# Graph attention before a diffusion layer: adjacency fetched by row tile in the second head group, row sums later and in quarters, SP and ScalarE in written order

## The chip, the cores and the metric

One core of a Trainium2 chip. The engines are TensorE (PE, its weight loads PEld), VectorE (DVE), ScalarE (ACT) and GpSimd (POOL); SyncE (SP) issues DMA transfers. Each runs its own instructions in the order in which they stand in its queue, and a waiting instruction holds what stands behind it. The metric is the device time of one execution in microseconds. Before the change it is 3462.85 us, the median of three executions (3461.5 to 3477.28).

## The reference

Two graph layers on 2708 nodes with 512 features and a dense 0/1 adjacency of 2708 x 2708 floats. The first is graph attention with 8 heads of 64:

```python
h = relu(layernorm(x)); feats = einsum('nf,hfd->hnd', h, W)
dense = leaky(e_self[:, :, None] + e_neigh[:, None, :]) + NEG_INF * (1 - adj)
x = x + relu(einsum('hnm,hmd->hnd', softmax(dense), feats) + b)
```

The second (two steps of diffusion) needs S = adj + I, the sums of its rows and of its columns, and a nucleus-sampled attention of its own. What follows concerns the first layer, and three things that the first layer makes for the second while it has the adjacency at hand: S in memory (`s_d`), row sums and column sums.

## The kernel before

**Tiles.** The nodes make NT = 22 row tiles of P = 128 (the last has 20). The attention stage works on the transposed adjacency: rows m are neighbours, columns n are the nodes that get an output. The columns are cut into four chunks (`tchunks`) of TC = 6 tiles, 768 columns (WC); the last chunk has 404. The 8 heads make two groups (`hgroups`) of four.

**The main loop.** For each chunk, for each head group, for each row tile t: VectorE makes four tiles e (L477), one per head, as max(r_b, kk) times a_c, where r_b holds the shares of the chunk's columns, spread over all partitions, kk is a number per neighbour and head, and a_c is the adjacency of this row tile and chunk in bf16. TensorE multiplies them by the features fw (L483) into six PSUM banks, `po`, which accumulate over all 22 row tiles. There are exactly six banks in the pool, so the next group can start in a bank only after ScalarE has copied that bank to `o_t` (L490). There are seven buffers for e, so VectorE can be almost two row tiles ahead of TensorE.

**The fetch of a chunk** (L444 to L459), once per chunk, used by both groups: SP loads the 128 x 768 piece of the transposed adjacency into a_f (L452, four buffers); ScalarE copies it to a_c (L454, NT + 2 = 24 buffers) and adds up the column sums on the way; where the row tile lies in the chunk itself, GpSimd adds the identity to the diagonal block of a_f (L458); SP stores a_f to `s_d` (L459). Where the last chunk or the last tile leaves columns or rows over, GpSimd clears them first (L449, L451).

**r_b** (`shares`, L353) is a load of four rows, spread to 128 partitions: 1536 KB, two buffers.

**The row sums** (`row_sums`, L337): for each row tile two halves of 1354 columns of the adjacency, loaded by SP into one buffer (L345) and added up by ScalarE (L346); GpSimd adds the halves and notes rows without any neighbour (`lone`, L347 to L349). `lone` is needed when the tile is finished, and the sums for the scales `rinv` and `ratio` (L514 to L517), which the second layer uses.

**Finishing a tile** (`finished`, L359) is cut into stages: transpose `o_t` (L372), divide (`shared`), add x and take the moments (`normed`), `cleared`, `asked`, `answered`. They use all engines. The dictionary `later` gives each stage and each row sum a row tile of the main loop, counted over both groups (key gi * NT + t), after whose matmuls it is written: tile i of a chunk is finished at keys 3i to 3i + 6 of the next chunk, so in that chunk's first group. The last chunk's four tiles are finished after the loop. Row sums of a chunk's tiles stand at keys NT + 3i, in the chunk's second group.

**What sets the order.** In this stage a planner orders the instructions of each engine from its own estimate of times, so the order on an engine is not the written one: it hoists loads, and it puts the fetch of the following chunk among the second group's work, since the program does not forbid it. The two steps of the second layer stand in a block (L1296) with a written order on four engines.

Of the kernel before, what the change touches and what calls it, by code (L numbers as in the profile page):

```python
# [9 lines left out]
F32 = mybir.dt.float32  # L10
BF16 = mybir.dt.bfloat16
# [3 lines left out]
AF = mybir.ActivationFunctionType  # L15
# [10 lines left out]
P = 128  # L26
# [28 lines left out]
def kernel(  # L55
# [163 lines left out]
    with ExitStack() as l0:  # L219
# [116 lines left out]

        def row_sums(t):  # L337
            pr = rows[t]
            half = small.tile([P, 2], F32, name="half")
            w = -(-N // 2)  # L340
            for i in range(2):
                arow = adjp.tile([P, w], F32, name="arow", bufs=1)
                c = slice(i * w, min((i + 1) * w, N))
                arow = arow[:pr, :c.stop - c.start]
                nc.sync.dma_start(out=arow, in_=adj[cols[t], c])  # L345
                nc.scalar.activation(arow, arow, AF.Copy, accum_out=half[:pr, i:i + 1])  # L346
            nc.gpsimd.tensor_tensor(rsum[:pr, t:t + 1], half[:pr, 0:1], half[:pr, 1:2], op=OP.add)  # L347
            nc.gpsimd.tensor_scalar(lone[:pr, t:t + 1], rsum[:pr, t:t + 1], 0.0, None, op0=OP.is_equal)
            nc.gpsimd.tensor_scalar(lone_n[:pr, t:t + 1], lone[:pr, t:t + 1], float(N), None, op0=OP.mult)  # L349

# [85 lines left out]

        later = {}
        unasked = []
        for ci, tiles in enumerate(tchunks):
            n0, n1 = tiles[0] * P, min((tiles[-1] + 1) * P, N)  # L440
            cw = n1 - n0
            r_bs = [shares(grp, n0, cw) for grp in hgroups[:1]]
            a_c = []
            for t in range(NT):  # L444
                pr = rows[t]
                a_f = adjp.tile([P, WC], F32, name="a_f", bufs=4)
                wide = len(tiles) * P
                if pr < P:
                    nc.gpsimd.memset(a_f, 0.0)  # L449
                elif cw < wide:  # L450
                    nc.gpsimd.memset(a_f[:, cw:wide], 0.0)  # L451
                nc.sync.dma_start(out=a_f[:pr, :cw], in_=adj_t[cols[t], n0:n1])  # L452
                a_c.append(adjp.tile([P, WC], BF16, name="a_c", bufs=NT + 2))
                nc.scalar.activation(a_c[t][:pr, :cw], a_f[:pr, :cw], AF.Copy,  # L454
                                     accum_out=cpart[:pr, t, ci:ci + 1])
                if t in tiles:
                    d = slice(t * P - n0, t * P - n0 + pr)
                    nc.gpsimd.tensor_tensor(a_f[:pr, d], a_f[:pr, d], ident[:pr, :pr], op=OP.add)  # L458
                nc.sync.dma_start(out=s_d[t * P:(t + 1) * P, n0:n0 + wide], in_=a_f[:, :wide])  # L459
            for i, t in enumerate(tiles):  # L460
                later.setdefault(NT + 3 * i, []).append(lambda t=t: row_sums(t))
            r_bs += [shares(grp, n0, cw) for grp in hgroups[1:]]
            o_t = work.tile([P, NG, len(beside), WC], F32, name="o_t", bufs=1)
            halfs = -(-cw // 512)
            hw = -(-cw // halfs)
            parts = [(a, min(a + hw, cw)) for a in range(0, cw, hw)]
            w = P // HG
            for gi, (grp, r_b) in enumerate(zip(hgroups, r_bs)):
                po = [[ps_o.tile([P, 512], F32, name="po") for _ in parts] for _ in beside]
                for t in range(NT):  # L470
                    pr = rows[t]
                    es = []
                    for k, slots in enumerate(beside):
                        while len(es) <= max(i for i, _ in slots):
                            i = len(es)
                            es.append(tp.tile([P, WC], F32, name="e", bufs=7))
                            nc.vector.scalar_tensor_tensor(es[i][:pr, :cw], r_b[:pr, i, :cw],  # L477
                                                           kk[:pr, t, grp[i]:grp[i] + 1],
                                                           a_c[t][:pr, :cw], op0=OP.max, op1=OP.mult)
                        for n, (a, b) in enumerate(parts):  # L480
                            for q, (i, d) in enumerate(slots):
                                of = fw[:pr, t, grp[i], d:min(d + w, DV)]
                                nc.tensor.matmul(po[k][n][q * w:(q + 1) * w, :b - a],  # L483
                                                 lhsT=of if d < DH else of.to_broadcast([pr, w]),
                                                 rhs=es[i][:pr, a:b], start=(t == 0), stop=(t == NT - 1))
                    for stage in later.pop(gi * NT + t, ()):
                        stage()
                for k in range(len(beside)):
                    for n, (a, b) in enumerate(parts):
                        nc.scalar.copy(o_t[:, gi, k, a:b], po[k][n][:, :b - a])  # L490

            final = ci == len(tchunks) - 1
            for i, t in enumerate(tiles):
                if final and i < 3:
                    bank = lambda g: ps_o.tile([P, 512], F32, name="po")
# [990 lines left out]
```

## Time and profile before

The profile is of one execution of 3462.71 us; its span from first to last instruction is 3460.9 us.

| | |
|---|---|
| time, median of three | 3462.85 us |
| profiled execution | 3462.71 us, span 3460.9 us |
| busy: TensorE, VectorE | 3183.6 us (92%), 2573.5 us (74%) |
| busy: ScalarE, GpSimd | 1502.3 us (43%), 933.6 us (27%) |
| mean granted TensorE clock | 0.973 |
| attention matmuls (L483), first to last start | 139.5 to 923.0 us |
| e (L477) | 704, 659.7 us |
| copies of adjacency (L454), first to last start | 88, 137.5 to 768.0 us |
| row sums on ScalarE (L346), first to last start | 44, 188.1 to 480.6 us |
| SP's load of r_b (L353) | 8, 64.9 to 775.9 us |

Times within the profile count from the first instruction. A line of the page's groups gives the source line, the engine, the operation with output and inputs, how many there were, their busy time and mean duration, and after the second bar how long the engine was idle just before them and what ended most of that. A line of a timeline gives the start, the duration (of several that are merged, from the first start to the last end), the engine and line, and in brackets the idle time ahead and what ended it. "SPq" lines are issues of DMA transfers, not the transfers themselves. TensorE runs a float32 matmul as two records.

### The profile page before, as it was taken

To read this page: it belongs to the slowest core of one execution; us is meant where nothing else is said; L and a number is where in the kernel's file an instruction comes from. 1 tells how busy PE (TensorE), PEld (TensorE's weight loads), DVE (VectorE), ACT (ScalarE), POOL (GpSimd) and SP (SyncE) were. 2 spreads that over 40 slices of the span, in tenths; PEclk is the share of its full clock that TensorE was granted. 3 is DMA by queue.
4 is the path that set the end of the run, shared out by engine and by line. 5 is a ranking of instruction groups with operands and counts; after the bars stand their busy time and mean duration, and the time that the engine had idled before them with its cause. 6 is when DMAs were issued, how large, how long until landed. Compare 5 with 4: busy or idle time off the path is not lost. (4 is left out here: it accounts for less than half of the span.)

```text
span 3460.9 us, 44356 instructions
## 1 busy us (share of the span) xinstructions
PE 3183.6 (92%) x16033; PEld 1695.6 (49%) x16033; DVE 2573.5 (74%) x4485; ACT 1502.3 (43%) x2219; POOL 933.6 (27%) x1091
## 2 busy tenths in 40 slices
PE   7988899998888999999999998899988999998998
PEld 4543333332455446455564643555555555555553
DVE  4588899899857564463745634997999899898893
ACT  2333231111046766665657622346544564455510
POOL 4221743607221222122122312111321233122211
PEclk9998999999999999999999999999999999999999
DMA  4478554222386245254453534865544653556553
GB/s 135 153 240 271 188 176 146 85 93 87 114 291 222 92 143 206 67 187 165 140 181 122 199 124 141 281 220 189 188 137 139 207 200 125 175 182 220 182 178 123
DMA packets 240046, 580.65 MB, mean 168 GB/s; under 512 B 32863, under 2 KB 66107, under 8 KB 239657
## 3 DMA queue, kind: packets, MB, share of 16 engines
q1 hardware_dynamic: 217721, 503.38, 43.9%
q0 software_dynamic: 22064, 74.09, 5.6%
q8 instruction: 127, 2.08, 0.2%
q14 instruction: 134, 1.10, 0.1%
HBM read 471.68 MB, written 105.68 MB: 167 GB/s over the span
## 5 line engine op out<-in xcount | busy, mean ns | idle before, releaser
L1168 PE MATMUL a<-va,at 128*128 128x512 f32 (+2 forms) x1936 | 887.2, 598 | 4.7 <-ACT at L1150 4.6
L483 PE MATMUL po<-e,fw 128*32 128x384 f32 (+3 forms) x7392 | 675.7, 502 | 65.7 <-DVE e L477 38.7
L477 DVE SCALAR_TENSOR_TENSOR e<-r_b,kk,a_c 128x768 f32<-128x768 f32 (+3 forms) x704 | 659.7, 997 | 50.4 <-PE po L483 41.8
L604 ACT ACTIVATE junk_a<-p,nth 128x2708 uint8<-128x2708 f32 (+1 forms) x240 | 612.7, 2553 | 38.1 <-POOL nth L619 33.6
L1042 PE MATMUL q<-hl,s_r 128*128 128x512 f32 x1936 | 541.5, 426 | 70.8 <-DMA s_r<-s_d 49.8
L1168 PEld LDWEIGHTS a<-va,at 128*128 128x128 f32 (+2 forms) x1936 | 338.2, 186 | 373.8 <-issue 341.4
L1042 PEld LDWEIGHTS q<-hl,s_r 128*128 128x128 f32 x1936 | 365.1, 193 | 235.5 <-issue 67.2
L483 PEld LDWEIGHTS po<-e,fw 128*32 128x32 f32 (+1 forms) x7392 | 256.9, 112 | 449.7 <-issue 260.0
L1150 ACT COPY at<-t 128x512 f32<-128x512 f32 (+3 forms) x308 | 140.9, 478 | 652.4 <-PE t L1146 648.6
L683 DVE SCALAR_TENSOR_TENSOR junk<-p,th 128x2708 bf16<-128x2708 f32 (+1 forms) x132 | 407.3, 3086 | 3.0
L1062 PE MATMUL q<-u_k,v 128*128 128x512 f32 x704 | 316.9, 592 | 1.1 <-ACT v L1052 1.1
L1045 PE MATMUL q<-s_r,hl 128*128 128x512 f32 (+1 forms) x1056 | 279.7, 409 | 17.7 <-DMA s_r<-s_d 15.1
L1045 PEld LDWEIGHTS q<-s_r,hl 128*128 128x128 f32 x1056 | 193.2, 189 | 97.7 <-issue 49.9
L1062 PEld LDWEIGHTS q<-u_k,v 128*128 128x128 f32 x704 | 133.3, 190 | 158.9 <-issue 154.2
L570 PE MATMUL t<-keys,q_t 128*128 128x452 f32 x528 | 158.7, 424 | 52.4 <-ACT p L572 50.6
L572 ACT COPY p<-t 128x452 f32<-128x452 f32 (+2 forms) x264 | 131.5, 537 | 172.0 <-PE t L570 128.0
L879 DVE MAX8 vn<-keep 128x8 f32<-128x2708 f32 (+1 forms) x66 | 196.8, 2981 | 2.3
L597 DVE TENSOR_REDUCE nmx<-p 128x1 f32<-128x2708 f32 (+1 forms) x44 | 130.5, 2967 | 63.9 <-ACT p L572 63.9
L1215 PE MATMUL a<-u_k,v_t 128*128 128x512 f32 (+1 forms) x352 | 170.2, 624 | 4.7 <-ACT yo L1222 3.0
L155 POOL TENSOR_SCALAR ln_rs<-ln_mv 128x1 f32<-128x1 f32 x66 | 49.6, 752 | 412.8 <-DVE ln_mv L154 411.5
L1146 PEld LDWEIGHTS t<-ident,keep 128*128 128x128 f32 (+1 forms) x968 | 115.5, 139 | 77.5 <-issue 48.0
L1146 PE MATMUL t<-ident,keep 128*128 128x128 f32 (+1 forms) x968 | 146.0, 273 | 3.5 <-ACT p L572 2.8
(311 smaller groups left out, 3435.3 us busy)
## 6 DMA issues: line engine op xcount, KB each, us to landing
hl<-vhl_d SPq DMA_DIRECT2D x132, 512.0 KB
s_r<-s_d SPq DMA_DIRECT2D x264, 256.0 KB
hl<-fhl_d SPq DMA_DIRECT2D x132, 512.0 KB
hl<-bhl_d SPq DMA_DIRECT2D x132, 512.0 KB
u_k<-in_L_gnn_U_dram SPq DMA_DIRECT2D x184, 256.0 KB
arow<-in_adj_dram SPq DMA_DIRECT2D x42, 677.0 KB
s_d<-a_f SPq DMA_DIRECT2D x66, 384.0 KB
s_r<-s_d SPq DMA_DIRECT2D x132, 192.0 KB
```

The costliest lines, as they stand in the source:

```text
L477: nc.vector.scalar_tensor_tensor(es[i][:pr, :cw], r_b[:pr, i, :cw], kk[:pr, t, grp[i]:grp[i] + 1], a_c[t][:pr, :cw], op0=OP.max, op1=OP.mult)
L483: nc.tensor.matmul(po[k][n][q * w:(q + 1) * w, :b - a], lhsT=of if d < DH else of.to_broadcast([pr, w]), rhs=es[i][:pr, a:b], start=(t == ...
L570: nc.tensor.matmul(pl[:, :c1 - c0], lhsT=q[:, i], rhs=self.keys[:, c0:c1], start=(i == 0), stop=(i == 1))
L604: nc.scalar.activation(junk[:pr], self.p[i][:pr], func, **kw)
L683: nc.vector.scalar_tensor_tensor(self.junk_b[:pr], p, th, p, op0=OP.is_ge, op1=OP.mult, accum_out=dst)
L879: v.max(vs, keep[0][:pr])
L1042: nc.tensor.matmul(half[j], lhsT=s_r[:, j * P:(j + 1) * P], rhs=hl[:, h], start=(c == 0 and h == 0), stop=(c == NT - 1 and h == 1))
L1045: nc.tensor.matmul(half[j][:, :w], lhsT=hl[:, h, j * P:(j + 1) * P], rhs=s_r[:, :w], start=(c == 0 and h == 0), stop=(c == NT - 1 and h == 1))
L1062: nc.tensor.matmul(half[j], lhsT=across_t[-1][k][:, j * P:(j + 1) * P], rhs=u_k, start=(start and k == 0), stop=(start and k == KD - 1))
L1146: nc.tensor.transpose(pt[:rows[c], j, :pr], keep[i][:pr, cols[c]], ident[:pr, :pr])
L1168: nc.tensor.matmul(pa[:pr], lhsT=at[:rows[c], j, :pr], rhs=va[:rows[c], c, :], start=(c == 0), stop=(c == NT - 1))
L1215: nc.tensor.matmul(pz[i][:rows[t]], lhsT=v_t[i][:, k, :rows[t]], rhs=u_k, start=(k == 0), stop=(k == KD - 1))
```

## The change

Four things. `row_sums` takes quarters of 677 columns with two buffers instead of halves with one, with one more addition on GpSimd. The fetch becomes a function for one row tile: all 22 tiles of chunk 0 are fetched ahead of its first group, and each further chunk's tile t is fetched after row tile t of the second group of the chunk ahead of it. The row sums move: in chunks 0 to 2 the chunk's first tile at key 2 NT - 4 = 40 (row tile 18 of the second group), its other tiles at keys 3i + 1 of the following chunk; the last chunk's own tiles stay at NT + 3i. The load of r_b is written one group ahead, after the first chunk's fetch for the second group. And SP and ScalarE keep the written order until the end of the stage; the other engines are still ordered by the planner.

```diff
@@ -336,15 +336,17 @@
 
         def row_sums(t):
             pr = rows[t]
-            half = small.tile([P, 2], F32, name="half")
-            w = -(-N // 2)
-            for i in range(2):
-                arow = adjp.tile([P, w], F32, name="arow", bufs=1)
+            n = 4
+            some = small.tile([P, n], F32, name="some")
+            w = -(-N // n)
+            for i in range(n):
+                arow = adjp.tile([P, w], F32, name="arow", bufs=2)
                 c = slice(i * w, min((i + 1) * w, N))
                 arow = arow[:pr, :c.stop - c.start]
                 nc.sync.dma_start(out=arow, in_=adj[cols[t], c])
-                nc.scalar.activation(arow, arow, AF.Copy, accum_out=half[:pr, i:i + 1])
-            nc.gpsimd.tensor_tensor(rsum[:pr, t:t + 1], half[:pr, 0:1], half[:pr, 1:2], op=OP.add)
+                nc.scalar.activation(arow, arow, AF.Copy, accum_out=some[:pr, i:i + 1])
+            nc.gpsimd.tensor_tensor(some[:pr, :2], some[:pr, :2], some[:pr, 2:], op=OP.add)
+            nc.gpsimd.tensor_tensor(rsum[:pr, t:t + 1], some[:pr, 0:1], some[:pr, 1:2], op=OP.add)
             nc.gpsimd.tensor_scalar(lone[:pr, t:t + 1], rsum[:pr, t:t + 1], 0.0, None, op0=OP.is_equal)
             nc.gpsimd.tensor_scalar(lone_n[:pr, t:t + 1], lone[:pr, t:t + 1], float(N), None, op0=OP.mult)
 
@@ -436,36 +438,61 @@
 
         later = {}
         unasked = []
+        spans = [(tiles[0] * P, min((tiles[-1] + 1) * P, N)) for tiles in tchunks]
+        a_cs = [[] for _ in tchunks]
+        r_bs = [[] for _ in tchunks]
+
+        def fetched(ci, t):
+            n0, n1 = spans[ci]
+            tiles, cw, pr = tchunks[ci], n1 - n0, rows[t]
+            a_f = adjp.tile([P, WC], F32, name="a_f", bufs=4)
+            wide = len(tiles) * P
+            if pr < P:
+                nc.gpsimd.memset(a_f, 0.0)
+            elif cw < wide:
+                nc.gpsimd.memset(a_f[:, cw:wide], 0.0)
+            nc.sync.dma_start(out=a_f[:pr, :cw], in_=adj_t[cols[t], n0:n1])
+            a_c = adjp.tile([P, WC], BF16, name="a_c", bufs=NT + 2)
+            a_cs[ci].append(a_c)
+            nc.scalar.activation(a_c[:pr, :cw], a_f[:pr, :cw], AF.Copy, accum_out=cpart[:pr, t, ci:ci + 1])
+            if t in tiles:
+                d = slice(t * P - n0, t * P - n0 + pr)
+                nc.gpsimd.tensor_tensor(a_f[:pr, d], a_f[:pr, d], ident[:pr, :pr], op=OP.add)
+            nc.sync.dma_start(out=s_d[t * P:(t + 1) * P, n0:n0 + wide], in_=a_f[:, :wide])
+
+        def shared_by(ci, gi):
+            n0, n1 = spans[ci]
+            r_bs[ci].append(shares(hgroups[gi], n0, n1 - n0))
+
+        gat = l0.enter_context(tc.manual_schedule(engines={SP, ACT}))
         for ci, tiles in enumerate(tchunks):
-            n0, n1 = tiles[0] * P, min((tiles[-1] + 1) * P, N)
+            n0, n1 = spans[ci]
             cw = n1 - n0
-            r_bs = [shares(grp, n0, cw) for grp in hgroups[:1]]
-            a_c = []
-            for t in range(NT):
-                pr = rows[t]
-                a_f = adjp.tile([P, WC], F32, name="a_f", bufs=4)
-                wide = len(tiles) * P
-                if pr < P:
-                    nc.gpsimd.memset(a_f, 0.0)
-                elif cw < wide:
-                    nc.gpsimd.memset(a_f[:, cw:wide], 0.0)
-                nc.sync.dma_start(out=a_f[:pr, :cw], in_=adj_t[cols[t], n0:n1])
-                a_c.append(adjp.tile([P, WC], BF16, name="a_c", bufs=NT + 2))
-                nc.scalar.activation(a_c[t][:pr, :cw], a_f[:pr, :cw], AF.Copy,
-                                     accum_out=cpart[:pr, t, ci:ci + 1])
-                if t in tiles:
-                    d = slice(t * P - n0, t * P - n0 + pr)
-                    nc.gpsimd.tensor_tensor(a_f[:pr, d], a_f[:pr, d], ident[:pr, :pr], op=OP.add)
-                nc.sync.dma_start(out=s_d[t * P:(t + 1) * P, n0:n0 + wide], in_=a_f[:, :wide])
-            for i, t in enumerate(tiles):
-                later.setdefault(NT + 3 * i, []).append(lambda t=t: row_sums(t))
-            r_bs += [shares(grp, n0, cw) for grp in hgroups[1:]]
+            final = ci == len(tchunks) - 1
+            if ci == 0:
+                shared_by(0, 0)
+                for t in range(NT):
+                    fetched(0, t)
+            if final:
+                for i, t in enumerate(tiles):
+                    later.setdefault(NT + 3 * i, []).append(lambda t=t: row_sums(t))
+            else:
+                later.setdefault(2 * NT - 4, []).append(lambda t=tiles[0]: row_sums(t))
+            if ci:
+                for i, t in enumerate(tchunks[ci - 1][1:]):
+                    later.setdefault(3 * i + 1, []).append(lambda t=t: row_sums(t))
+            a_c = a_cs[ci]
             o_t = work.tile([P, NG, len(beside), WC], F32, name="o_t", bufs=1)
             halfs = -(-cw // 512)
             hw = -(-cw // halfs)
             parts = [(a, min(a + hw, cw)) for a in range(0, cw, hw)]
             w = P // HG
-            for gi, (grp, r_b) in enumerate(zip(hgroups, r_bs)):
+            for gi, grp in enumerate(hgroups):
+                if gi + 1 < NG:
+                    shared_by(ci, gi + 1)
+                elif not final:
+                    shared_by(ci + 1, 0)
+                r_b = r_bs[ci][gi]
                 po = [[ps_o.tile([P, 512], F32, name="po") for _ in parts] for _ in beside]
                 for t in range(NT):
                     pr = rows[t]
@@ -485,11 +512,12 @@
                                                  rhs=es[i][:pr, a:b], start=(t == 0), stop=(t == NT - 1))
                     for stage in later.pop(gi * NT + t, ()):
                         stage()
+                    if gi == NG - 1 and not final:
+                        fetched(ci + 1, t)
                 for k in range(len(beside)):
                     for n, (a, b) in enumerate(parts):
                         nc.scalar.copy(o_t[:, gi, k, a:b], po[k][n][:, :b - a])
 
-            final = ci == len(tchunks) - 1
             for i, t in enumerate(tiles):
                 if final and i < 3:
                     bank = lambda g: ps_o.tile([P, 512], F32, name="po")
```

## The prediction

> **What bounds the kernel now.** The change touches only the attention stage, so I cut the span at that stage first. The groups of instructions place its matmuls (L483) from 139.5 to 923 us. The page shows who is costly there:
>
> ```profile
> L483 PE MATMUL po<-e,fw 128*32 128x384 f32 (+3 forms) x7392 | 675.7, 502 | 65.7 <-DVE e L477 38.7
> ...
> L477 DVE SCALAR_TENSOR_TENSOR e<-r_b,kk,a_c 128x768 f32<-128x768 f32 (+3 forms) x704 | 659.7, 997 | 50.4 <-PE po L483 41.8
> ```
>
> Both engines are nearly full, and the idle time is small in total: 65.7 us of TensorE. Its place matters more than its sum. The second view is busy time per stretch, cut where one head group ends and the next begins (columns: stretch, then busy us and count of PE, PEld, DVE, ACT, POOL, then granted clock, DMA share, GB/s):
>
> ```profile
> 139.50:227.00 87.50, 87.47 (x1056) 49.20 (x1056) 86.49 (x92) 29.69 (x57) 20.47 (x16) 0.98 0.83 288
> 227.00:239.30 12.30, 0.03 (x4) 0.03 (x5) 2.52 (x3) 4.06 (x8) 0.63 (x3) 0.53 0.56 189
> 239.30:328.00 88.70, 88.70 (x1056) 32.44 (x1056) 82.25 (x86) 35.00 (x68) 18.98 (x25) 0.96 0.77 254
> 328.00:346.00 18.00, 4.22 (x32) 1.06 (x32) 2.06 (x3) 8.42 (x18) 0.94 (x5) 0.50 0.91 288
> 346.00:475.30 129.30, 114.35 (x1133) 46.01 (x1133) 110.83 (x147) 39.23 (x67) 92.94 (x103) 0.95 0.56 183
> ...
> 477.30:564.20 86.90, 86.90 (x1058) 31.90 (x1057) 83.48 (x90) 23.56 (x52) 13.66 (x20) 0.98 0.56 180
> 564.20:690.40 126.20, 114.82 (x1156) 46.24 (x1156) 113.59 (x148) 12.61 (x28) 78.65 (x74) 0.96 0.25 88
> ```
>
> A group without finishing work takes 86.9 us and TensorE is full: 3.95 us for each of 22 row tiles. A first group of chunks 1 and 2 also finishes the chunk before and takes 129.3 and 126.2 us; VectorE and GpSimd set that. Two holes stand out, of 12.3 us after the first group and about 18 us after the second. At 564.2 there is no hole. The timeline of ScalarE before the first hole's end gives the cause, and TensorE's line the result:
>
> ```profile
> 237.43 1.33 ACT L346 ACTIVATE arow<-arow 128x1354 f32<-128x1354 f32 x1 [4.28 <-DMA arow<-in_adj_dram]
> ...
> 238.76 1.98 ACT L490 COPY o_t<-po 128x384 f32<-128x384 f32 x5
> ...
> 239.27 12.95 PE L483 MATMUL po<-e,fw 128*32 128x384 f32 x124 [12.28 <-ACT o_t L490]
> ```
>
> All six accumulation banks belong to the finished group, and their copies (L490) stood behind row sums that waited for their own loads. The second hole is the same queue: three copies at 340.87, three at 345.42, row sums between and ahead of them.
>
> Last I looked at how quickly a load and a store alternate on SP, since that is the order that the new code writes down. SyncE's timeline in chunk 1's second group:
>
> ```profile
> 495.78 0.33 SPq L459 DMA_DIRECT2D s_d<-a_f  x1
> 496.20 0.38 SPq L452 DMA_DIRECT2D a_f<-in_adj_t_dram  x1
> 499.61 0.33 SPq L459 DMA_DIRECT2D s_d<-a_f  x1
> 500.03 0.38 SPq L452 DMA_DIRECT2D a_f<-in_adj_t_dram  x1
> 503.55 0.33 SPq L459 DMA_DIRECT2D s_d<-a_f  x1
> ```
>
> Each store waits until its load has landed, each load is issued 0.42 us after the store ahead of it: 3.83 and 3.94 us per tile, just TensorE's 3.95. In the first group the old order escapes this: four, later three loads are issued in a row, then their stores. The tiles on the diagonal have a longer way. ScalarE and GpSimd, chunk 2's fetch:
>
> ```profile
> 517.48 0.85 ACT L454 ACTIVATE a_c<-a_f 128x768 bf16<-128x768 f32 x1 [2.93 <-DVE e L477]
> ...
> 518.50 1.12 POOL L458 TENSOR_TENSOR a_f<-a_f,ident 128x128 f32<-128x128 f32 x1 [33.95 <-ACT a_c L454]
> ...
> 519.65 0.33 SPq L459 DMA_DIRECT2D s_d<-a_f  x1
> ```
>
> The store follows 2.1 us after ScalarE began its copy, because the addition of the identity writes what ScalarE reads.
>
> **What the Trainium skill says.** "DMA: Bandwidth & Descriptors", section "Anatomy of one DMA": a wait for a semaphore is served on the issuing sequencer, not by the DMA engines. So a store that waits holds back every later load of SP; the 3.4 us gaps above agree. The same section gives a DMA some 2 us of fixed cost besides its bytes: a 384 KB load here took 3.02 us unhindered, of which 1.15 us is data at the 341 GB/s of the busiest stretch, so 1.9 us. "TensorE: Matmul & The Clock Gate", Part 1: about 3.4 us of work at half clock after an idle time; the trace has weight loads 0.64 us apart after 239.27 and 0.32 us from 245 on, so 5.7 us. "SBUF — State Buffer", "two separate sides": a GpSimd operation and a VectorE operation with two SBUF inputs exclude each other; e (0.95 us alone) took up to 2.06 us here.
>
> **The change part by part.**
> (a) Row sums leave chunk 0, but for one tile late in its second group. The copies of the first group then find ScalarE free, and the first hole's cause goes.
> (b) Fetching in written order, one tile at a time. A plain tile: from load to store the five undisturbed ones took 3.02, 3.08, 4.42, 3.41 and 3.52 us, mean 3.49; with 0.42 us to the next load 3.9 us. A diagonal tile: 3.9 + 2.1 = 6.0 us, six per chunk.
> Chunk 0 is fetched while its own first group eats it. From the first copy at 137.5 us, tile 21 is there at 137.5 + 6×6.0 + 15×3.9 = 232.0; its copy 0.9, a first e 0.95 and 3.84 us of matmuls end the group at 237.7, against 227.0 before.
> (c) r_b of group 2 is now behind all 22 fetches on SP; before it was loaded at 68.8 us. Issued at 232.5, behind the last store, 1.57 MB at 341 GB/s = 4.6 us with 2.3 us around it and 1.1 us for the store: there at 240.6. One e later TensorE starts, at 241.7: a hole of 4 us instead of 12.3, and the group starts 2.4 us *later* than before (239.3).
> (d) The next chunk's fetch, inside the second group. SP first has the load of r_b, which waits for the last e of the first group (call this S), then the fetches. From S: r_b and first tile 1.97 MB, 5.8 + 2.3 = 8.1 us; 15 plain tiles 58.5; 6 diagonal ones 36; the row sum at tile 18, of which SP waits for two quarters, 5.4 (first quarter landed 3.3, ScalarE 0.77 and 0.86 for two, an estimate along the line from 404 elements in 0.54 us to 1354 in 1.33 us, issue 0.4); last copy 0.9: 108.9 us. Only then come the copies of the banks, in the program's order. What hides it is the second group: from S (473.5 in chunk 1) to its end (564.2) 90.7 us. Excess: 18.2 us.
> At chunk 0 to 1, S is 236.7, and r_b of group 2 is still moving (1.6 us): the copies start at 347.2, TensorE at 347.7. Before, allowing for the three matmul groups done early, it stood as if it had started at 344. So +3.7 us up to here.
> At chunk 1 to 2 there was no hole: +18.
> At chunk 2 to 3 loads are 202 KB (2.45 us to the store, cycle 3.0) and four tiles are diagonal, 1.85 us more each: 5.5 + 17×3.0 + 4×4.85 + 5.4 − 3.0 + 0.7 = 79 us, within 90: 0. If it were not, it would cost its excess.
> (e) Row sums move out of chunk 1's first group (eighteen tiles down to five): 129.3 to 126.2, −3.1; the slow copies at 475.3 go, −1.3. They move into the first groups of chunks 2 and 3, five each, four GpSimd operations per tile instead of three. GpSimd is on the path there: 20 operations of 0.2 to 0.85 us, about half of it felt, +2 each, +4; bounds 0 and +10. ScalarE is held about 5.8 us by each, one in three tiles of 5.7 us; its next finishing step comes two tiles on, so hidden. VectorE's rsum, rinv and ratio at the end: under 2 us, not counted.
> Sum: 3.7 − 3.1 − 1.3 + 18 + 4 = +21.3 us. The profiled execution took 3462.71 us (span 3460.9), which is the median 3462.85 to 0.2 us: 3484.
>
> Unknown from here: whether the very first r_b stays at 64.9 us or falls behind the stage's start; that adds 0 or 4.6 us, and I take 0.
>
> **The rivals.**
> 1. *The fetch keeps pace.* With 3.0 us per plain tile, as the 202 KB loads have it, and little for the diagonal, (d) is under 90 us, both holes go: the second group would start at 233.8, chunk 1 at 321 instead of 344, −23, with (e)'s −4.4 it is 3436. Against it: three of five waits above are over 3.4 us. This is the one on the other side; it decides where the chain falls below 90.7 us.
> 2. *Half way.* Every load as quick as the two at 3.02 and 3.08 us: cycle 3.44, diagonal 5.2 with the 0.66 us addition seen once; chain 96.6, excess 6. Chunk 0's first group ends at 233.8, chunk 1 starts at 328 (−16); −16 + 6 − 4.4 + 4 = −10: 3453.
> 3. *Row sums stall the finishing work.* GpSimd waits in its order for a quarter that comes late, VectorE for GpSimd (L401 waited 20.3 us in all for L397). Some 2 us for each of 10 row sums, over (d): 3504. Chunk 1's first group, with three times as many, was only 3 us longer than chunk 2's, so I hold it small.
> If every load were as late as the 4.42 us one, the chain would be 129 us and the total near 3540; that is the far end.
>
> **How the numbers follow.** Forecast 0.58, rival 1 0.14, rival 2 0.18, rival 3 0.10. Half a per cent, 17.3 us, is about what a measurement can tell from no change. Of the forecast's cases 0.45 lie above 3480 and 0.13 within; rival 3 is slower; rival 2 is 0.10 within and 0.08 faster; rival 1 faster. So faster 0.22, same 0.23, slower 0.55. The forecast's own range is 3470 to 3510; to leave out no more than 2 in 10 it reaches to rival 2 and a part of rival 1, and to the slower loads: 3445 to 3520.
>
> **What would show it.** The hole after group 1 shrinks to some 4 us and ends on r_b, not on ScalarE. A hole of 15 to 20 us appears where chunk 1 ends, its copies released behind an a_c copy that waited for its load; the one at chunk 0's end stays. SP's stores wait for loads in all of it, the mean cycle near 3.9 and 6.0 us. VectorE waits for a_c in the first six tiles. The prediction is wrong if TensorE runs through the end of chunk 1, or if SP issues the next load before the store.

## The result, and the profile after

The changed kernel takes 3511.61 us, the median of four executions (3509.74 to 3513.09), against 3462.53 us for the kernel before on the same chip: a ratio of 1.0129, 95% interval 1.0106 to 1.0151. The forecast was 3484 us. It is slower as forecast, and by 49.1 us between the medians where 21.3 were worked out (by the ratio some 45 us; one of the four executions of the kernel before took 3477.28 us).

The page of the changed kernel, its groups of instructions (line, engine, operation, count, then busy us and mean ns, then idle time ahead and what ended it):

```profile
L510 PE MATMUL po<-e,fw 128*32 128x384 f32 (+3 forms) x7392 | 695.0, 509 | 83.9 <-DVE e L504 62.2
L504 DVE SCALAR_TENSOR_TENSOR e<-r_b,kk,a_c 128x768 f32<-128x768 f32 (+3 forms) x704 | 656.2, 990 | 75.1 <-PE po L510 48.4
```

TensorE has the same 7392 records, with 18 us more idle time in front of them and 19 us more busy time. (L510 was L483, L504 was L477.) As before, the place matters more. Busy time per stretch, cut where a head group begins (stretch, then busy us and count of PE, PEld, DVE, ACT, POOL, then granted clock, DMA share, GB/s):

```profile
139.50:242.40 102.90, 99.15 (x1056) 39.86 (x1057) 85.17 (x89) 22.54 (x48) 4.83 (x7) 0.96 0.56 185
242.40:350.40 108.00, 88.97 (x1062) 59.80 (x1062) 89.77 (x96) 24.43 (x54) 6.02 (x11) 0.90 0.54 178
350.40:486.90 136.50, 118.85 (x1162) 47.85 (x1163) 112.51 (x146) 29.17 (x71) 87.82 (x95) 0.94 0.42 141
486.90:591.90 105.00, 90.48 (x1062) 33.44 (x1062) 84.84 (x90) 26.13 (x59) 9.53 (x18) 0.89 0.53 173
591.90:727.50 135.60, 120.74 (x1162) 48.60 (x1163) 111.96 (x146) 29.10 (x71) 88.48 (x96) 0.92 0.41 138
727.50:825.60 98.10, 93.71 (x1081) 33.55 (x1081) 83.28 (x96) 22.07 (x64) 11.77 (x30) 0.93 0.43 134
```

The second groups of chunks 0 and 1 (second and fourth line) now take 108 and 105 us where TensorE has some 90 us of work. The first groups of chunks 1 and 2 (third and fifth) take 136 us, and GpSimd is busy for 88 of them. (The last stretch runs 4 us into the next group.) The DMA engines were busy for 0.56 of chunk 0's first group, 0.83 before, so it is not their bandwidth that spaces the loads.

For a common measure, here is each group from the end of the last copy of its predecessor's banks to the end of the last copy of its own, for both kernels. (The expectations quoted below cut the groups less evenly; some of their times differ from those given here by 1 to 6 us.)

| group (us) | before | after | difference | forecast |
|---|---|---|---|---|
| chunk 0, both, end at | 346.6 | 352.2 | +5.6 | +3.7 |
| chunk 1 first | 131.0 | 136.5 | +5.5 | -4.4 |
| chunk 1 second | 87.2 | 105.0 | +17.8 | +18 |
| chunk 2 first | 127.5 | 135.6 | +8.1 | +2 |
| chunk 2 second | 87.3 | 92.6 | +5.3 | 0 |
| chunk 3 first | 95.7 | 102.9 | +7.2 | +2 |
| chunk 3 second | 49.0 | 50.8 | +1.8 | 0 |
| sum | 924.4 | 975.7 | +51.3 | +21.3 |

What follows these groups gave back 2.7 us of the span. That remainder took between 2531 and 2552 us in all the runs below, so effects of a few us are read from the groups and not from the total.

The hole at the end of chunk 0, from the timeline of the changed kernel:

```profile
346.15 0.33 SPq L461 DMA_DIRECT2D s_d<-a_f  x1
...
346.21 0.84 ACT L457 ACTIVATE a_c<-a_f 128x768 bf16<-128x768 f32 x1 [2.87 <-DMA a_f<-in_adj_t_dram]
...
349.00 0.33 SPq L461 DMA_DIRECT2D s_d<-a_f  x1
...
349.08 0.84 ACT L457 ACTIVATE a_c<-a_f 20x768 bf16<-20x768 f32 x1 [1.93 <-DMA a_f<-in_adj_t_dram]
...
349.93 1.19 ACT L519 COPY o_t<-po 128x384 f32<-128x384 f32 x3
...
350.43 0.87 PE L510 MATMUL po<-e,fw 128*32 128x384 f32 x4 [9.26 <-ACT o_t L519]
```

The second group's matmuls had ended at 330.0; the banks are copied 20 us later, because the copies stand behind the last a_c copy of the next chunk's fetch, and that one waited for its load. SP's own waits between 125 and 1000 us, in the changed kernel (us in total, times, longest):

```profile
SPq L461 <- DMA a_f<-in_adj_t_dram: 274.6, 88, 8.5
SPq L346 <- ACT arow L347: 267.7, 76, 36.2
SPq L355 <- DVE e L504: 104.2, 4, 47.7
SPq L461 <- POOL a_f L460: 44.3, 22, 5.1
```

All 88 stores waited for a load, 3.1 us each. In the kernel before it was 60, and 2.0 us each:

```profile
SPq L459 <- DMA a_f<-in_adj_t_dram: 118.7, 60, 7.0
```

### The profile page after: what moved, and what is told of

It reads as the page before. It is cut to its first block, busy times and chain, and to the rows that moved or that the text cites. A ratio compares the mean times of both kernels' runs of the same rounds, so it can differ in the third digit from the quotient of the medians.

```text
span 3509.5 us, 44598 instructions
## 1 busy us (share of the span) xinstructions
PE 3213.8 (92%) x16033; PEld 1719.8 (49%) x16033; DVE 2571.6 (73%) x4485; ACT 1513.1 (43%) x2307; POOL 934.2 (27%) x1113
## 5 line engine op out<-in xcount | busy, mean ns | idle before, releaser
L510 PE MATMUL po<-e,fw 128*32 128x384 f32 (+3 forms) x7392 | 695.0, 509 | 83.9 <-DVE e L504 62.2
L504 DVE SCALAR_TENSOR_TENSOR e<-r_b,kk,a_c 128x768 f32<-128x768 f32 (+3 forms) x704 | 656.2, 990 | 75.1 <-PE po L510 48.4
L510 PEld LDWEIGHTS po<-e,fw 128*32 128x32 f32 (+1 forms) x7392 | 272.5, 113 | 469.0 <-issue 256.2
L457 ACT ACTIVATE a_c<-a_f 128x768 bf16<-128x768 f32 (+1 forms) x88 | 67.7, 770 | 288.8 <-DMA a_f<-in_adj_t_dram 251.3
```

The source lines that it names most:

```text
L510: nc.tensor.matmul(po[k][n][q * w:(q + 1) * w, :b - a], lhsT=of if d < DH else of.to_broadcast([pr, w]), rhs=es[i][:pr, a:b], start=(t == ...
```

## The experiments

The theory for the holes: load, wait and store alternate on SP, the copies of the banks stand behind the fetch on ScalarE. Its rival: what the holes cost is mainly the slow restart of TensorE after them. For the first groups the theory is that row sums delay the finishing work through GpSimd; its rivals are the loads and ScalarE's sums, and the holes themselves.

**Stores two tiles late.** The load of the next tile no longer stands behind a store that waits.

```diff
+        owed = []
+        LAG = 2
-            nc.sync.dma_start(out=s_d[t * P:(t + 1) * P, n0:n0 + wide], in_=a_f[:, :wide])
+            owed.append(lambda: nc.sync.dma_start(out=s_d[t * P:(t + 1) * P, n0:n0 + wide], in_=a_f[:, :wide]))
+            while len(owed) > (LAG if t < NT - 1 else 0):
+                owed.pop(0)()
```

> The changed kernel with one edit: SP's store of a row tile is written two row tiles later, so two loads are under way before a store waits. ScalarE's order is as it was. If SP's chain of load, wait, store is what fills the second groups, a tile costs SP about 2.4 us (0.77 MB at some 340 GB/s) instead of 3.9 or 6.0, the fetch ends before the group does, and the holes ahead of chunks 1 and 2 (20 and 16 us) go to under 2 us; the first group of chunk 0 falls from 102.9 us to about 88, its second from 108 to 88, the second of chunk 1 from 105 to 87. The first groups of chunks 1 and 2 lose another 5 us each if half-clock restart after a hole is what lengthened them (136.5 and 135.6 us); about 1 us if it was the row sums. In all about 3430 us. If instead ScalarE's written order holds the bank copies, with the a_c copies ahead of them, holes of over 10 us stay and the time is above 3490.

Measured: 3458.56 us, ratio to before 0.9985 (0.9974 to 0.9996). Both holes are gone; chunk 0 ended at 314.8 us instead of 352.2, and the second groups of chunks 1 and 2 took 87.5 us. TensorE's line through chunk 0:

```profile
140.70 177.55 PE L514 MATMUL po<-e,fw 128*32 128x384 f32 x2160 [5.88 <-DVE e L508]
```

So the chain on SP made the holes. The first groups stayed at 137.2 and 137.3 us: they had not been long because of the holes ahead of them, and the part of the expectation that rested on that (to 3430) fell. "DMA: Bandwidth & Descriptors" of the Trainium skill (Anatomy of one DMA) has waits served on the issuing sequencer; this run shows the price here, some 50 us for a store written two tiles too early.

**No addition on the diagonal.** The lines that add the identity are left out.

```diff
-            if t in tiles:
-                d = slice(t * P - n0, t * P - n0 + pr)
-                nc.gpsimd.tensor_tensor(a_f[:pr, d], a_f[:pr, d], ident[:pr, :pr], op=OP.add)
```

> The changed kernel without the addition of the identity on the diagonal tiles (this part is not computed). If the chain of load, wait and store on SP sets both holes with the lengths of the prediction, each diagonal tile falls from 6.0 to 3.9 us: the chain of chunk 1's and of chunk 2's fetch is 12 us shorter, the holes of 20 and 16 us fall to about 8 and 4, chunk 0's first group ends some 5 to 9 us earlier: total near 3512 - 24 - 7 = 3481. If the holes come from the row sum near the end or from the load of r_b, they shorten by under 4 us each: total above 3500.

Measured: 3476.67 us, ratio 1.0043 (1.0026 to 1.006). Between the groups' matmuls the hole at the end of chunk 0 fell from 20.4 to 9.7 us, that at the end of chunk 1 from 16.3 to 10.2, and chunk 0's first group ended 9.3 us earlier (233.0 against 242.3). TensorE around the first two ends:

```profile
233.51 89.63 PE L507 MATMUL po<-e,fw 128*32 128x384 f32 x1056 [1.06 <-DVE e L501]
332.79 6.52 PE L507 MATMUL po<-e,fw 128*32 128x384 f32 x48 [8.81 <-ACT o_t L516]
```

A hole also depends on how far TensorE is behind VectorE when the chain begins. The chain itself, from SP's load of r_b to the first bank copy, shows in two lines of the changed kernel, here for the fetch of chunk 2:

```profile
479.58 0.38 SPq L355 DMA_DIRECT2D r_b<-en_d  x1
...
591.43 2.30 ACT L519 COPY o_t<-po 128x384 f32<-128x384 f32 x6
```

It takes 112.0 us for chunk 1's fetch and 111.9 for chunk 2's, and 102.6 and 103.3 without the addition. The diagonal tiles' longer way is thus 9.4 and 8.6 us of it, some 1.5 us a tile where 2.1 were expected. The rest is mostly the plain chain.

**The second group's r_b earlier in chunk 0.**

```diff
                 for t in range(NT):
                     fetched(0, t)
+                    if t == NT // 2:
+                        shared_by(0, 1)
...
                 if gi + 1 < NG:
-                    shared_by(ci, gi + 1)
+                    if ci:
+                        shared_by(ci, gi + 1)
```

> The changed kernel, but in chunk 0 the load of r_b for the second group is written after row tile 11 instead of behind all 22 fetches. If the prediction's term (c) holds, the hole of 4 us between chunk 0's two groups goes, as the fetch is one load of 5 us later on SP in its middle: the first group ends up to 5 us later or, where TensorE is behind the fetch by less, as much later as the second group starts earlier: between 0 and -4 us on the total, 3508 to 3512. If the hole has another cause (the copies of the banks, or a_c), it stays at 3 to 4 us and the total is 3512 to 3516.

Measured: 3521.25 us, ratio 1.0155 (1.0123 to 1.0187). TensorE now runs through the boundary, but it gets there 5 us later, since the load stands in the middle of the fetch instead of at its end:

```profile
224.60 37.83 PE L513 MATMUL po<-e,fw 128*32 128x384 f32 x432
```

Chunk 0 ended at 356.7 us instead of 352.2. The wait that r_b caused was in the end 0.7 us of TensorE, not 4, and moving it cost more than it held. The stage ended 3.9 us later in all; the rest of the 10 us between the medians is not in these groups.

**No row sums at all, and row sums without their GpSimd operations.** In the first kernel `row_sums` does nothing; in the second it loads and lets ScalarE add up, and the four operations after that are left out.

```diff
-            nc.gpsimd.tensor_tensor(some[:pr, :2], some[:pr, :2], some[:pr, 2:], op=OP.add)
-            nc.gpsimd.tensor_tensor(rsum[:pr, t:t + 1], some[:pr, 0:1], some[:pr, 1:2], op=OP.add)
-            nc.gpsimd.tensor_scalar(lone[:pr, t:t + 1], rsum[:pr, t:t + 1], 0.0, None, op0=OP.is_equal)
-            nc.gpsimd.tensor_scalar(lone_n[:pr, t:t + 1], lone[:pr, t:t + 1], float(N), None, op0=OP.mult)
```

> The changed kernel without the row sums: their loads, ScalarE and GpSimd work are left out and the sums are set to 1, so this part isn't computed. If the row sum at row tile 18 costs SP's chain 5.5 us, the holes ahead of chunks 1 and 2 shrink by 5 to 6 us each, and the last groups by 3 together. The first groups of chunks 1 and 2 fall by 1 to 2 us each if half-clock restart lengthened them, by 5 to 8 if the row sums on ScalarE and GpSimd did. So about 3494 us against about 3482.

> The changed kernel with the row sums' loads and their ScalarE sums kept, but without the four small GpSimd operations that follow them for each tile (rsum, lone and lone_n are set once; this part is not computed). With all of it the first groups of chunks 1 and 2 take 136.4 and 135.5 us from bank copy to bank copy, without row sums 127.8 and 128.7. Theory 1: the GpSimd operations, and what stands behind them, cost the 8 us: near 128 and 129, total near 3497. Theory 2: the loads and ScalarE cost them (ScalarE is held, SP blocked, the DMA rings shared): near 136 and 135, total near 3511.

Measured: 3484.58 us, ratio 1.0048 (1.0025 to 1.007), and 3496.92 us, ratio 1.0088 (1.006 to 1.0117). The executions of the second spread from 3484.01 to 3510.13 us, so it is read from its groups. The first groups of chunks 1 to 3 took 127.8, 128.8 and 101.5 us without row sums, and 129.0, 129.4 and 97.6 with loads and ScalarE sums but without GpSimd's part. With everything they take 136.5, 135.6 and 102.9. So in chunks 1 and 2 nearly the whole of it is GpSimd's 20 small operations; the loads and ScalarE's quarters cost about 1 us. In chunk 3 the two kernels differ by 3.9 us the wrong way round, so its share is not settled. The holes stayed in both, of 14 and 15 us without row sums and of 20 and 21 us without GpSimd's part; without row sums the chain from the load of r_b to the first bank copy was 5.2 and 4.5 us shorter, near the 5.4 us that the prediction gave the row sum in it.

Not all of the 7.5 us in chunk 1 is time gained. SP loads r_b, and so begins the next fetch, when VectorE has finished its last e of the first group, and the hole follows from that fetch: chunk 1's second group took 109.3 us in the kernel without GpSimd's part, 105.0 in the changed one, and the two groups together 238.3 against 241.5.

**Halves again, and quarters with two GpSimd operations.** Is it the number of operations, or the quarters?

```diff
# halves
-            n = 4
+            n = 2
-                arow = adjp.tile([P, w], F32, name="arow", bufs=2)
+                arow = adjp.tile([P, w], F32, name="arow", bufs=1)
-            nc.gpsimd.tensor_tensor(some[:pr, :2], some[:pr, :2], some[:pr, 2:], op=OP.add)
# quarters, two operations
-            nc.gpsimd.tensor_tensor(some[:pr, :2], some[:pr, :2], some[:pr, 2:], op=OP.add)
-            nc.gpsimd.tensor_tensor(rsum[:pr, t:t + 1], some[:pr, 0:1], some[:pr, 1:2], op=OP.add)
+            nc.scalar.activation(some[:pr], some[:pr], AF.Copy, accum_out=rsum[:pr, t:t + 1])
```

> The changed kernel with the row sums in halves with one buffer as before, and so three GpSimd operations for a tile instead of four. Theory 1 (GpSimd's operations lengthen the first groups, about in proportion to their time): of 7.5, 6.2 and 5.3 us a quarter to a third goes, about -2 us in each, and the holes grow by 1 to 3 us, as SP is blocked by a half of 4 us instead of by two quarters: total near 3508. Theory 2 (the number does not matter, but that finishing steps wait for late sums): halves come later than quarters, first groups +1 to +3 each: total near 3520.

> The changed kernel with its quarters, but the four partial sums are added by one ScalarE operation, so that two GpSimd operations are left for a tile (lone and lone_n) instead of four. If the number of GpSimd operations lengthens the first groups, and not the size or the lateness of the loads, the first groups of chunks 1, 2 and 3 (136.4, 135.5 and 102.1 us with four, 131.4, 130.6 and 98.4 with halves and three) are at or below those of the halves: near 130, 130 and 98, total near 3500. If quarters as such cost the 5 us by which halves were shorter, they stay near 136, 135 and 102, total near 3511.

Measured: 3503.89 us, ratio 1.0097 (1.0067 to 1.0126), and 3507.73 us, ratio 1.0119 (1.0098 to 1.014). First groups of chunks 1 to 3: 130.1, 129.6 and 99.2 us with halves and three operations; 134.0, 132.9 and 100.2 with quarters and two. The halves gave back 6.4 and 6.0 us in chunks 1 and 2 where 2 were expected. The two operations gave back 2.5 and 2.7, which is no more than kernels with the same four operations differ by: chunk 1's first group took 133.0 us in the one with r_b earlier. How far TensorE lags at the group's end does not enter if one measures from the first copy of the banks to the end of VectorE's last e. This, and VectorE's wait for `ln_rs`, the scale of the layer norm that GpSimd makes for its `shift`, in the first groups of chunks 1 and 2:

| GpSimd operations for a row sum | to the last e (us) | wait for `ln_rs` (us) |
|---|---|---|
| none | 124.0, 124.3 | 2.3, 2.3 |
| three, halves | 126.2, 125.0 | 2.5, 2.5 |
| two, quarters | 128.1, 127.2 | 3.8, 4.1 |
| four, quarters, r_b earlier | 128.5, 129.3 | 5.2, 5.2 |
| four, quarters (the change) | 129.6, 128.9 | 5.2, 5.2 |

The number alone does not order them; the wait for `ln_rs` does. What the profile shows beside it is the order in which the planner puts these operations among the finishing work. GpSimd and VectorE in the changed kernel, one tile of chunk 1's first group:

```profile
402.41 0.58 POOL L410 DMA_DIRECT2D xb_d<-xt  x1 [0.30 <-POOL xt L409]
...
402.95 2.84 DVE L504 SCALAR_TENSOR_TENSOR e<-r_b,kk,a_c 128x768 f32<-128x768 f32 x3
403.01 0.97 POOL L348 TENSOR_TENSOR some<-some 128x2 f32<-128x2 f32 x1
...
403.96 0.98 POOL L155 TENSOR_SCALAR ln_rs<-ln_mv 128x1 f32<-128x1 f32 x1
...
404.92 0.91 POOL L349 TENSOR_TENSOR rsum<-some 128x1 f32<-128x1 f32 x1
...
405.80 0.57 POOL L156 TENSOR_TENSOR ln_rs<-ln_rs,nhalf 128x1 f32<-128x1 f32 x1
...
406.40 0.16 DVE L417 SCALAR_TENSOR_TENSOR shift<-ln_mv,ln_rs 128x1 f32<-128x1 f32 x1 [0.61 <-POOL ln_rs L156]
```

The same place with halves:

```profile
405.57 0.57 POOL L409 DMA_DIRECT2D xb_d<-xt  x1 [0.30 <-POOL xt L408]
406.28 0.89 POOL L155 TENSOR_SCALAR ln_rs<-ln_mv 128x1 f32<-128x1 f32 x1
407.25 1.19 POOL L156 TENSOR_TENSOR ln_rs<-ln_rs,nhalf 128x1 f32<-128x1 f32 x1
408.43 0.59 POOL L348 TENSOR_TENSOR rsum<-some 128x1 f32<-128x1 f32 x1
```

With four operations two stand ahead of the two that make `ln_rs`; with halves they stand behind. VectorE's `shift`, its next operation of the tile, waits for `ln_rs`. Each of the first three operations here lasts about as long as one of VectorE's three e (2.84 us together) and ends 0.04 to 0.08 us after one. The waits in chunk 1's first group, changed kernel, then the one without GpSimd's part:

```profile
PE po L510 <- DVE e L504: 16.5, 14, 3.3
...
DVE shift L417 <- POOL ln_rs L156: 5.2, 5, 1.7
```

```profile
PE po L510 <- DVE e L504: 11.4, 14, 1.5
...
DVE shift L417 <- POOL ln_rs L156: 2.3, 5, 0.5
```

VectorE waits 2.9 us more for `ln_rs`, and TensorE 5.1 us more for e. That goes with most of the 7.5 us, but the placement was not changed by itself, so it is argued and not shown, and how much each place is worth is open.

**VectorE's sums behind the last e.** The reduction of the column sums and the scales are ordered behind the last e of the stage.

```diff
-                            nc.vector.scalar_tensor_tensor(es[i][:pr, :cw], r_b[:pr, i, :cw],
+                            last_e = nc.vector.scalar_tensor_tensor(es[i][:pr, :cw], r_b[:pr, i, :cw],
...
+        with tc.issue_after(last_e.ins):
             if NFULL:
                 nc.vector.tensor_reduce(csum[:, :NFULL], cpart[:, :NFULL, :], axis=AX.X, op=OP.add)
```

(The same for the lines of `rinv` and `ratio`.)

> The changed kernel with VectorE's small work on the column and row sums (reduce, reciprocal, ratio) put behind its last e. The planner had put it among the e of the last two groups, where it waited 6.4 us for the last a_c of chunk 3 and 3.0 us for a row sum. If that wait is what lengthened chunk 2's second group (98.1 us against 87.0 before) and chunk 3's (54.6 against 51.5), they fall to 88 to 90 and 52: about 3500 us. If SP's fetch of chunk 3 is what ends late there, the copies of the banks still wait for it, the group stays above 95 us and the time at 3508 or more.

Measured: 3512.61 us, ratio 1.0127 (1.0096 to 1.0159). Chunk 2's second group fell from 92.6 to 87.5 us; chunk 3's did not (50.8 and 51.2). The changed kernel's timeline shows what it was:

```profile
799.68 5.66 PE L510 MATMUL po<-e,fw 128*32 128x384 f32 x68
...
808.00 0.24 DVE L533 TENSOR_REDUCE csum<-cpart 128x21 f32<-128x84 f32 x1 [6.36 <-ACT a_c L457]
...
809.73 2.79 PE L510 MATMUL po<-e,fw 128*32 128x384 f32 x16 [4.39 <-DVE e L504]
```

The planner had put a 0.24 us reduction ahead of the last tiles' e; it needs the column sums of the last full tile, so VectorE stood for 6.4 us and TensorE for 4.4. The stage ended 5.7 us earlier, and yet the total did not fall; where the second layer gave it back was not found.

**The move alone, and the order alone.** The kernel before with quarters and the later row sums, the planner's order kept (first); the kernel before with SP and ScalarE in the written order and nothing else (second).

```diff
# the order alone
+        gat = l0.enter_context(tc.manual_schedule(engines={SP, ACT}))
         for ci, tiles in enumerate(tchunks):
```

> The kernel before, in the planner's order and with its own fetch, with the row sums alone changed: in quarters, and one chunk later as in the changed kernel. If only row sums ahead of the bank copies made the two holes of the kernel before (12.3 and 18 us), both fall below 3 us and the half-clock restarts go too: about 3430 us. If the fetch in the planner's order makes a part of them, above all of the second, at least 8 us stay there: about 3442 us. If the planner places the later row sums as badly in chunks 2 and 3, no gain: 3460.

> The kernel before with SP and ScalarE in the program's order and nothing else of the change: each chunk's adjacency is fetched at its own start, row sums in the second group. Theory 1: no chain stands ahead of the copies of the banks, so the holes of 20 and 16 us are about 4 (one load, one copy, one e), while the first groups are set by the finishing work near 128 us and the fetch keeps ahead of it at 22 x 3.9 + 6 x 2.1 = 98 us: total near 3456. Theory 2: the fetch beside the finishing work is later than that (its copies stand behind ScalarE's finishing steps, its diagonal behind GpSimd's), first groups of 135 to 140 us: total near 3475 to 3485.

Measured: 3470.15 us, ratio 1.0013 (1.0003 to 1.0023), and 3555.03 us, ratio 1.0241 (1.0212 to 1.027). In the first the planner hoisted the row sums again, to 188 to 433 us, and the two old holes stayed (10.3 and 21.1 us of waiting on `o_t`). Where they end is the planner's matter as long as it has the queue. In the second the second groups had no such hole (87.5 us), but the first groups of chunks 1, 2 and 3 took 157.5, 174.6 and 132.0 us, far over both expectations. ScalarE in chunk 1's first group, with the order alone:

```profile
417.50 0.84 ACT L455 ACTIVATE a_c<-a_f 128x768 bf16<-128x768 f32 x1 [2.95 <-DVE e L478]
...
420.34 0.84 ACT L455 ACTIVATE a_c<-a_f 20x768 bf16<-20x768 f32 x1 [1.91 <-DMA a_f<-in_adj_t_dram]
...
436.44 0.81 ACT L416 ACTIVATE v<-o,shift,ln_rs 128x512 f32<-128x512 f32 x1 [15.16 <-DVE shift L415]
```

The group had begun at 335.3. All 22 copies stand ahead of the first finishing step on ScalarE, as the loads of x for the finishing stand behind all 22 fetches on SP: the first tile's v comes 101 us into the group. The written order alone is thus worse than the whole change; the fetch by row tile repairs what it breaks, and leaves the chain behind. The fetch by row tile in the planner's order was not run.

**Two versions from this.** Both have the stores two tiles late. One puts the row sums back into the second group of their own chunk:

```diff
+            for i, t in enumerate(tiles):
+                later.setdefault(NT + 3 * i, []).append(lambda t=t: row_sums(t))
```

> Stores two row tiles late as in e1_lag, and every row sum in quarters in the second group of its own chunk, where the kernel before has them. If SP's blocking on the quarters is hidden by the loads issued ahead: no hole, first groups near 128 instead of 135, total near 3458 - 15 = 3443. If it adds to the chain of fetches: 22 tiles of 3.0 us, 6 more row sums of 5.4 us each, 8.1 us at the start, over 105 us against 90: holes of 15 us at the ends of chunks 0 and 1, less the 15 gained: total near 3473.

Measured: 3482.52 us, ratio 1.006 (1.004 to 1.008). First groups 130.9 and 130.4 us, near the 128 hoped for, but the second groups of chunks 0 and 1 took 107.5 and 103.7 us: SP, blocked 5.4 to 7.8 us by each row sum of chunk 0, is late with the fetch again. The other leaves the row sums where the change has them and takes GpSimd out of them:

```diff
-            nc.gpsimd.tensor_tensor(some[:pr, :2], some[:pr, :2], some[:pr, 2:], op=OP.add)
...
+            nc.scalar.activation(some[:pr], some[:pr], AF.Copy, accum_out=rsum[:pr, t:t + 1])
+            nc.vector.tensor_scalar(lone[:pr, t:t + 1], rsum[:pr, t:t + 1], 0.0, None, op0=OP.is_equal)
+            nc.vector.tensor_scalar(lone_n[:pr, t:t + 1], rsum[:pr, t:t + 1], 0.0, float(N), op0=OP.is_equal, op1=OP.mult)
```

> Stores two row tiles late as in e1_lag, row sums where the change has them, but what followed the quarters on GpSimd goes to ScalarE (one sum of the four) and VectorE (two flags). Theory 1 (GpSimd's part of the row sums is what lengthens the first groups): 135 falls to about 129 in chunks 1 and 2, total near 3447. Theory 2 (the loads and ScalarE's quarters): 135 stays, total near 3459.

Measured: 3438.11 us, ratio 0.9933 (0.9913 to 0.9952), faster than both kernels. Its stretches:

```profile
140.00:227.70 87.70, 87.70 (x1060) 49.07 (x1062) 86.57 (x92) 20.59 (x46) 5.63 (x7) 0.98 0.70 210
227.70:313.10 85.40, 85.40 (x1060) 34.32 (x1056) 83.68 (x91) 26.85 (x61) 6.33 (x7) 1.00 0.74 232
313.10:441.90 128.80, 115.22 (x1164) 48.45 (x1156) 112.39 (x159) 28.56 (x76) 77.96 (x74) 0.97 0.40 135
```

TensorE is full through chunk 0, and the first groups of chunks 1 and 2 take 130.7 and 131.9 us, where late stores alone left 137.2 and 137.3; in chunk 1's GpSimd is busy for 78 us instead of 88, with 74 operations instead of 95. The row sums and their flags are still made here, and the finishing still needs them, so it was not the finishing's wait for late row sums that cost the time. The gain on the kernel before is all in chunk 0, which ends at 313.6 us instead of 346.6; chunks 1 to 3 together are 7.5 us longer than there.

## Why the prediction was right in kind and short in size

**Right, with some luck: (d), the chain at the end of chunks 0 and 1.** The forecast had TensorE's start in chunk 1 at 347.7 us and chunk 1's second group 18 us longer; they came out at 350.4 and 17.8. Late stores removed both holes, and the profile shows the copies behind an a_c copy that waited for its load, as announced. From the load of r_b to the first bank copy the chain was reckoned at 110.5 and 108.9 us and took 112.0 and 111.9. Its row sum held (5.2 and 4.5 us for 5.4); its diagonal tiles were too dear (9.4 and 8.6 us for 12.6), and the plain part too cheap. That 17.8 so nearly met 18 is luck: the chain was 3 us longer, but it also began 7.4 us ahead of the second group's first matmul, where the forecast had 3.8. In the five other kernels with the same fetch and stores the hole at the end of chunk 1 was 19.8 to 22.1 us, in the changed kernel 16.3.

**Right by offsetting, (b) and (c).** Chunk 0's first group was to end at 237.7 us and a 4 us hole for r_b to follow. Its matmuls ended at 241.7: the fetch was 4 us slower than reckoned, so r_b was nearly there, and TensorE waited 0.7 us. The start at 242.4 was forecast as 241.7. The run with r_b earlier shows that the fetch was the limit.

**The step that failed: (e), the row sums in the first groups.** It put -4.4 us on chunk 1's first group and +2 each on those of chunks 2 and 3, -0.4 in all. They grew by 5.5, 8.1 and 7.2 us, 20.8 in all, so (e) holds 21 of the 30 us by which the groups exceed the forecast. Two mistakes stand in it.

It credited chunk 1 for having five row sums instead of eighteen (ten by GpSimd's operations there), as if their number set the cost. The kernel before spent 17.3 us on 30 such operations in chunk 1's first group and had none in chunk 2's, and yet the first was only 3.5 us longer; its waits for `ln_rs` were nearly the same, 3.3 and 3.1 us, where the changed kernel has 5.2.

And +2 is too little by the forecast's own figures: half of twenty operations of 0.2 to 0.85 us is 2 to 8.5 us, and it took the lowest. In chunk 1 the four kinds of operation take 4.4 + 3.7 + 2.1 + 3.1 = 13.3 us, 0.66 each. Without them the first groups are 7.5 us shorter in chunk 1 and 6.2 in chunk 2, and with the sums moved off GpSimd, both with late stores, 6.4 and 5.5; in chunk 3 it is between 1.4 and 5.3, by which of the two kernels one takes. So about half of their time is felt, as the prediction had it, and the size of one operation was wrong. This is rival 3 in its place, with GpSimd and not the late quarter as the cause (GpSimd waited 0.9 us for a quarter in this group), and on top of the forecast's holes. Its chance of 0.10 was too small: the argument against it, that chunk 1 with three times as many row sums was only 3 us longer, holds for the planner's placement of that kernel, not for a new one.

**Also wrong: "under 2 us, not counted" for VectorE's sums.** The price was right, the wait was missing. The planner put the reduction in front of the last e, where it waits for the last fetch: 5.1 of the 5.3 us in chunk 2's second group. The step of the working that hid it is (d)'s "0" for chunk 2 to 3. Its chain was also too short: the fetch ran from 720.3 to 812.9 us, 93 us against 79, and the row sum inside it took 15.1 us from the end of the store ahead of it to the next store, where 5.4 and one diagonal tile of 4.85 were counted. TensorE's group covered that; the reduction did not.

**Summed.** By the end of the stage, the kernel without GpSimd's operations is 18.8 us shorter than the changed one, and the kernel with VectorE's sums behind the last e 5.7. Less the 4 us that the forecast had counted for GpSimd, that is some 20 of the 30 us, if the two add up, which no run shows. The rest stays unassigned, and so does the second layer's share of a few us.

## What to carry to other kernels

A load, a store that waits for it, and the next load on one queue make a chain of the full latency: let stores trail by some tiles where buffers are to spare (here two tiles, of four buffers), and count what stands behind the last of them on other engines (here the copies that free the PSUM banks). A move that costs little on its own engine is priced at the engine that serves the dependent chain: count the small operations that come to stand between two links of it at what they take beside the work that runs there, and ask where a planner that keeps the other queues will put them. Where an order is written down on two engines, look for every operation that stands last in program order and first in need.

## What was unexpected in the hardware

The same GpSimd addition of one number per partition (L349) took 0.19 us once and 0.85 to 0.91 us four times in chunk 1's first group. What differs is the operation of VectorE beside it. Of the 32 operations of the row sums and of `ln_rs` there, 17 ended within 0.1 us after an e of VectorE and took 0.59 to 0.98 us; the ten with no VectorE operation beside them took 0.21 to 0.58 us. So the price of such an operation was mostly that of the e beside it, and two of them put ahead of a finishing step delay it by nearly 2 us. The prediction reckoned with this exclusion for e, not for the small operations.

And a pause of TensorE cost little where TensorE is not the limit: after a hole of 20 us chunk 1's first group took 136.5 us, and 137.2 with no hole ahead of it.
